# A fused convolution, attention and expert kernel: attention's sums are kept by channel and divided after a DRAM round trip, and three small turns move to VectorE

## The chip, the cores and the metric

The kernel runs on one core of a Trainium2 chip. The time is the device time of one execution in microseconds, as the median of the runs taken. A core has TensorE (PE, matrix products; weight loads are listed apart as PEld), VectorE (DVE), ScalarE (ACT, activations), GpSimd (POOL) and SyncE (SP), each with its own in-order queue. Here SP issues nearly all DMAs. TensorE writes to PSUM; VectorE and ScalarE read it from there.

## The reference

Layer 0 convolves twice, gates, and adds an attention with one head; layer 1 is attention with 16 heads of 8 channels, a gated feed-forward part and a router that mixes two of eight experts. All of it is float32.

```python
x: (4, 64, 64, 128)                       # 4 images, 4096 tokens, 128 channels
# layer 0
c1 = conv3x3(elu(x), W1) + b1;  c2 = conv3x3(c1, W2) + b2
a, b = split(c2);  c3 = a * sigmoid(b)
q, k, v = c3 @ Wq + bq, c3 @ Wk + bk, c3 @ Wv + bv       # 4, 4, 16 channels
probs = softmax(q k' / 4 under a strict lower triangle)
x = x + c3 + tile(probs @ v, 8) @ W3 + b3
# layer 1, t = tokens of x
h0 = ln(t)
q, k, v = h0 @ wq, h0 @ wk, h0 @ wv       # 16 heads of 8 channels
attn = softmax(q k') v                    # over all 4096 tokens of the image
h = h0 + attn @ wo
t = t + h + silu(h @ w1) * (h @ w3) @ w2
y = ln(t)
p = softmax(y @ router_w + router_b);  the two largest, scaled to sum 1, are the gates
t = t + sum over the chosen experts of gate * (y @ expert_w[e] + expert_b[e])
```

## The kernel before

**Names.** A chunk is 512 tokens (`QB`), 8 chunks to an image (`NQ`), 32 tiles of 128 keys (`NT`). The 16 heads of layer 1 are treated in four groups (`NG1`) of four slots (`NSLOT`), each slot having 32 partitions (`SLOT`).

**The long loop.** `attention_step` handles one tile of 128 keys for one chunk of queries and one group: 4096 steps in all. `scores()` issues four products (one per head, each on its own 32 rows of the array) into two PSUM tiles `s` (three buffers), and ScalarE exponentiates each tile of 128x1024 into `e`. `values()` issues four products with 9-column weights `vg` into the one accumulator `acc`: in each slot row 0 gathers the sum of the exponentials, rows 1 to 8 the weighted values. `values` run two steps behind `scores` (`finish(2)`).

After the last key tile VectorE copies `acc` to `at` (channels on partitions). Then `by_token` is put on the list `urgent`: TensorE turns `at` in four 128x128 transposes into PSUM tile `m`, VectorE takes the reciprocal of the sums (`rc`), multiplies (`nt`) and SP stores 32 channels per token in DRAM tensor `a`. With the last group, `last_part` is put on `fillers`.

**Fillers.** All other work is written as generators that yield a cost and a word; the main loop calls `insert` at most once per step, between the scores of the step and older values, as long as `credit` is above zero. The credit grows by a rate worked out from the work and steps left, and falls by the yielded cost. A yield of 0.0 is thus a pause of one step. `urgent` work goes first and counts 0.6. The list is served in order, one generator until it ends. The generators are `first_attention` (convolutions, first layer's attention, second layer's operands of the next image) and `last_part` (what follows attention, per chunk). All use the PSUM tile `m`, of which there is one; beside the loop, `product` cuts weights into 32 columns so that four products fill four column strips of the array. First-layer attention has its own steps (`first_step`) in the same loop.

`InOrder` keeps every engine's instructions in the order in which they are written.

**`last_part` before.** It loads `nt`, `h`, `t` for a chunk, pauses three steps, turns `nt` with four transposes, copies to `an`, multiplies by `wo1`, and goes on to the feed-forward part. After the second layer norm it turns `y`, multiplies by the router weights `rw` (four products with 128x128 weights, 8 columns moving), finds the gates on VectorE after an exponential `pr` on ScalarE, pauses four steps, turns the gates with four transposes into `g8` (experts on partitions), multiplies by the expert biases `eb`, and then forms all eight experts, `by_e`, in halves.

**First values before.** In `first_attention`, `wv0` is multiplied with `c3` as 128x128 weights and 16 moving columns, so that tokens are on partitions at once.

**Start and end.** Ahead of the loop (`alone`) the generators run beside each other without it, with `s` tiles for PSUM. The small weights are loaded by `weight(...)` in one run on SP's queue. After the loop the rest of the fillers runs alone: what is left of chunk 6 and all of chunk 7 of the last image.

All engine calls pass through one helper, so the profile gives one line number, L105, for all; the groups are told apart by tile names.

Of the kernel before, what the change touches and what calls it, by code (L numbers as in the profile page):

```python
# [15 lines left out]
P = 128  # L16
# [99 lines left out]
def fast_path(ctx: ExitStack, tc: tile.TileContext, a: dict, where: dict, out: bass.AP, verdict):  # L116
# [102 lines left out]
    seen = const.tile([P, 4, B], FP, name="f_seen")  # L219


    steps_in, undone, fillers, urgent = [], [], [], []
    held, turn = [False], [0]

    def do_step(step):
        scores, values = step
# [7 lines left out]
    def advance(part):  # L234

        r = next(part[0], None)
        part[1] = max(0.5, part[1] - (r[0] if r else 0.0))
        held[0] = r is not None and r[1] in ("held", "rounds")
        return r

    def insert():

        if urgent and not held[0] and turn[0] > urgent[0][0]:
            urgent.pop(0)[1]()
            return 0.6
        while fillers:
            r = advance(fillers[0])
            if r is not None:
                return r[0]
            fillers.pop(0)  # L250
        return 0.0
# [25 lines left out]
    def product(ps, lhsT, rhs, start=True, stop=True):  # L277

        m = lhsT.shape[1]
        size = m if alone[0] else SLOT  # L280
        for lo in range(0, m, size):
            hi = min(lo + size, m)
            pe.matmul(ps[lo:hi], lhsT=lhsT[:, lo:hi], rhs=rhs, start=start, stop=stop)

    def halves(ps, lhs, rhs, size=P):

# [240 lines left out]
    def first_attention(b, st):  # L527
# [3 lines left out]
        for c in range(NQ):  # L531
            while len(st.done) <= c:

                yield (0.0, "wait") if alone[0] else next(st.conv, (0.0, "stop"))
            while alone[0] and st.second < c - 1:
                yield 0.0, "wait"
            c3 = st.done[c]
            t = xt
            pool.tensor_tensor(by_k(t), by_k(t), b3.unsqueeze(1).to_broadcast([P, 4, C]), ALU.add)
            if c + 1 < NQ:  # L540
                xt = load_x(b, c + 1, "xt")

            ps = bank()
            yield from halves(ps, wq0, c3)
            u, qx0 = chunk("u"), chunk("qx0")
            dve.tensor_scalar(u, ps, bq0, 0.25, ALU.add, ALU.mult)
            dve.tensor_reduce(top0[:, 0, c : c + 1], u, AX.X, ALU.max, apply_absolute_value=True)
            two_terms(u, qx0, "q")
            yield 0.46, "stop"
            ps = bank()  # L550
            for j in range(NSLOT):
                pe.matmul(
                    ps[j * SLOT : (j + 1) * SLOT, :P],
                    lhsT=wk0,
                    rhs=c3[:, j * P : (j + 1) * P],
                    start=True,
                    stop=True,
                )
            yield 0.25, "held"
            for k in range(4):  # L560
                pe.matmul(
                    ps[:, P + k * DV0 : P + (k + 1) * DV0],
                    lhsT=c3[:, k * P : (k + 1) * P],
                    rhs=wv0,
                    start=True,
                    stop=True,
                )
            u = chunk("u")[:, :P]
            dve.tensor_scalar(u, ps[:, :P], bk0, None, ALU.add)
            v0c = v0[:, 4 * c : 4 * c + 4, 1 : 1 + DV0]  # L570
            dve.tensor_tensor(
                v0c,
                ps[:, P : P + 4 * DV0].rearrange("p (k s) -> p k s", s=DV0),
                bv0.unsqueeze(1).to_broadcast([P, 4, DV0]),
                ALU.add,
            )
            dve.tensor_reduce(top0[:, 1, c : c + 1], u, AX.X, ALU.max, apply_absolute_value=True)
            dve.tensor_reduce(
                top_v0[:, c : c + 1],
                v0[:, 4 * c : 4 * c + 4, :].rearrange("p k s -> p (k s)"),  # L580
                AX.X,
                ALU.max,
                apply_absolute_value=True,
            )
            two_terms(u, kx0[:, c, :], "k")
            yield 0.95, "stop"

            ps = bank()
            transposed(c3, ps)
            dve.tensor_tensor(t, ps, t, ALU.add)  # L590
            yield 0.6, "stop"

            while alone[0] and st.read < c:
                yield 0.0, "wait"
            sums, found = [], []
            for r in range(c + 1):
                steps_in.append(first_step(c, r, qx0, sums, found))
            while not found:
                yield 0.0, "rounds"
            st.ready.append((t, found[0]))  # L600
            while not alone[0] and st.second <= c:
                yield from second_operands(b, st)
# [173 lines left out]
    def attention_step(b, seg, kt, place, qx, vg, part):  # L776
# [19 lines left out]
        def values(es):  # L796
# [8 lines left out]
            if kt == seg.hi - 1:  # L805
                at = chunk("at1")
                if part:
                    dve.tensor_tensor(at, acc, part[0], ALU.add)
                else:
                    dve.tensor_copy(at, acc)  # L810
                if seg.hi == NT:
                    urgent.append((turn[0] + 1, lambda: by_token(b, g, c, at)))
                else:
                    sp.dma_start(out=scratch[b]["p"][g, c], in_=at)

        return scores, values

    def by_token(b, g, c, at):

        ps = m_tile()  # L820
        transposed(at, ps)
        pj = ps.rearrange("p (k j s) -> p k j s", j=NSLOT, s=SLOT)
        rc = sm.tile([P, 4, NSLOT], FP, tag="rc", name="rc")
        dve.reciprocal(rc, pj[:, :, :, 0])
        nt = sm.tile([P, 4, NSLOT, HD1], FP, tag="nt", name="nt")
        dve.tensor_tensor(
            nt, pj[:, :, :, 1 : 1 + HD1], rc.unsqueeze(3).to_broadcast([P, 4, NSLOT, HD1]), ALU.mult
        )
        gc = slice(g * NSLOT * HD1, (g + 1) * NSLOT * HD1)
        sp.dma_start(out=scratch[b]["a"][c][:, :, gc], in_=nt.rearrange("p k j d -> p k (j d)"))  # L830
        if g == NG1 - 1:
            fillers.append([last_part(b, c), LAST])


    def last_part(b, c):
        d = scratch[b]
        t, h, nt = chunk("xt", "t"), chunk("xe", "h"), chunk("pos", "nt")
        sp.dma_start(out=by_k(nt), in_=d["a"][c])
        sp.dma_start(out=h, in_=d["h"][c])
        sp.dma_start(out=t, in_=d["t"][c])  # L840
        for _ in range(3):
            yield 0.0, "stop"
        ps = bank()
        transposed(nt, ps)
        an = chunk("pos", "an")
        dve.tensor_copy(an, ps)
        yield 0.6, "stop"
        ps = bank()
        tokens(ps, an, wo1, range(2))
        yield 0.46, "held"  # L850
# [45 lines left out]
        dve.tensor_copy(yT, ps)  # L896
        yield 0.6, "stop"
        ps = bank()
        for k in range(4):
            pe.matmul(  # L900
                ps[:, k * NE : (k + 1) * NE], lhsT=yT[:, k * P : (k + 1) * P], rhs=rw, start=True, stop=True
            )
        shape = [P, 4, NE]

        def over(ap):
# [2 lines left out]
        def top(score, name):  # L908
# [10 lines left out]

        lg = small("lg", [4, NE])  # L920
        dve.tensor_tensor(
            lg, ps[:, : 4 * NE].rearrange("p (k e) -> p k e", e=NE), rb.unsqueeze(1).to_broadcast(shape), ALU.add
        )
        m0 = small("m0", [4])
        dve.tensor_reduce(m0, lg, AX.X, ALU.max)
        dve.tensor_tensor(lg, lg, over(m0), ALU.subtract)
        pr = small("pr", [4, NE])
        yield 0.95, "stop"
        act.activation(pr, lg, AF.Exp)
        yield 0.0, "stop"  # L930
        yield 0.0, "stop"
# [5 lines left out]
        dve.tensor_tensor(w1, w1, pr, ALU.mult)  # L937
        dve.tensor_tensor(m1, m1, m2, ALU.add)
        dve.reciprocal(m1, m1)
        gate = small("gate", [4, NE])  # L940
        dve.tensor_tensor(gate, w1, over(m1), ALU.mult)
        for _ in range(4):
            yield 0.0, "stop"

        ps = bank()
        for k in range(4):
            pe.transpose(ps[:NE, k * P : (k + 1) * P], gate[:, k, :], ident)
        g8 = chunk("at0", "g8")[:NE]
        dve.tensor_copy(g8, ps[:NE, :])
        yield 0.6, "stop"  # L950
        ps = bank()
        tokens(ps, g8, eb, range(2))
        yield 0.46, "held"
# [25 lines left out]
    class Batch:  # L979


        def __init__(self, b):
# [4 lines left out]
                "k": [P, 2, N],  # L987
                "q": [NQ, P, 2, 2, QB],
                "v": [NG1, P, NQ, 4 * NSLOT * (1 + HD1)],
                "a": [NQ, P, 4, C],  # L990
            }
            if b == 0:
                dims["p"] = [NG1, NQ, P, QB]
# [36 lines left out]
    def weight(name, src, shape):  # L1030
        w = const.tile(shape, FP, name="f_" + name)
        sp.dma_start(out=w, in_=src)
        return w


    n_row = 4 * DQK0

# [19 lines left out]
    wk0 = repeated("wk0", a["L0_conv_Wk"], 1)  # L1057
    bq0 = repeated_bias("bq0", a["L0_conv_bq"])
    bk0 = repeated_bias("bk0", a["L0_conv_bk"])
    wv0 = weight("wv0", a["L0_conv_Wv"], [P, DV0])  # L1060
    bv0 = weight("bv0", a["L0_conv_bv"].partition_broadcast(P), [P, DV0])
    b3 = weight("b3", a["L0_conv_b3"].partition_broadcast(P), [P, C])

# [16 lines left out]
    fw2 = const.tile([P, len(FCH), C], FP, name="f_fw2")  # L1080
    for n, (lo, size) in enumerate(FCH):
        sp.dma_start(out=fw2[:size, n, :], in_=a["L1_attn_w2"][lo : lo + size, :])
    rw = weight("rw", a["L1_ffn_router_w"], [P, NE])
    rb = weight("rb", a["L1_ffn_router_b"].partition_broadcast(P), [P, NE])
    we = weight("we", a["L1_ffn_expert_w"].rearrange("e d c -> d e c"), [P, NE, C])
    we_f = we.rearrange("p e c -> p (e c)")
# [100 lines left out]
    steps = stream()  # L1187
    credit, waiting = 0.0, False
    while True:
        turn[0] += 1  # L1190
        if steps_in:
            do_step(steps_in.pop(0))
        else:
# [15 lines left out]
            within = steps_left[b] - 40 if b + 1 < B else min(steps_left[b] - 40, 160)  # L1209
            rate = sum(us for _, us in fillers) / max(1, within)  # L1210
        credit = min(0.7, credit + rate)
        if waiting or credit > 0.0 and not quiet[0] or urgent and not held[0]:
            credit -= insert()
        finish(2)
    finish(0)
    while urgent:
        if held[0]:
            advance(fillers[0])
        else:
            urgent.pop(0)[1]()  # L1220
    alone[0] = True
    run_alone([(r for part in fillers for r in part[0])], lambda: False)

# [716 lines left out]
```

## Time and profile before

| | us |
|---|---|
| median of 3 runs | 8293.93 (8293.24 to 8297.26) |
| profiled execution, whole | 8302.43 |
| its span | 8300.7 |

Busy time of the engines in the span, by stretch (start of the span to 415 us: start; to 8225: the loop; then the tail):

| stretch | PE | DVE | ACT | POOL |
|---|---|---|---|---|
| 415 to 8225 (7810 us) | 7746.7 | 2272.6 | 7727.6 | 559.0 |
| whole span (8300.7 us) | 8073.1 | 2557.3 | 7915.4 | 708.5 |

TensorE's granted clock is 0.98 of full speed over the span and 1.00 in the loop. A group's row of the profile gives line, engine, operation, out<-in by the program's names, shapes and count, then busy time and mean duration in ns, then idle time ahead of it with what ended it. A pipelined matmul's duration overlaps that of its neighbours, so time per step is read from start to start. The groups that the change touches:

```profile
L105 ACT ACTIVATE e<-s 128x1024 f32<-128x1024 f32 x8424 | 7813.0, 1088 | 132.6 <-PE s L105 123.5 <-ACT e L105 1.5 <-issue 1.5
L105 PE MATMUL m<-f_consts,at 128*128 128x128 f32 x512 | 84.0, 287 | 1.2 <-DVE at L105 1.2
L105 PE MATMUL m<-f_rw,y2T 128*128 128x8 f32 x248 | 32.8, 259 | 0.0
L105 PE MATMUL m<-f_wv,c 128*128 128x16 f32 x240 | 32.1, 266 | 0.0
L105 PE MATMUL m<-f_consts,nt 128*128 128x128 f32 x124 | 20.4, 288 | 3.3 <-DMA nt<-d_a 3.0
L105 PE MATMUL m<-f_consts,gate 128*8 128x128 f32 x124 | 18.6, 273 | 0.0
```

The DMAs near it, with size and median time from issue to landing:

```profile
d_a<-nt SPq DMA_DIRECT2D x128, 64.0 KB, 2.1
nt<-d_a SPq DMA_DIRECT2D x32, 256.0 KB, 2.9
h<-d_h SPq DMA_DIRECT2D x32, 256.0 KB, 3.1
```

### The profile page before, as it was taken

The page shows a single profiled execution, that of the slowest core. Times are in us where ns is not written, and L with a number is a line of the kernel's source. Part 1 is how long each engine was busy: PE and PEld are TensorE (multiplying, and loading weights), DVE is VectorE, ACT ScalarE, POOL GpSimd, SP SyncE. Part 2 cuts the span into 40 slices and gives each one's busy share as a digit, 9 for nine tenths or more (in the row PEclk, how much of TensorE's full clock was granted, in tenths as well). Part 3 has the DMA queues.
Part 4 walks back from the last instruction along what each step waited for, and adds up shares of the span by engine and source line. Part 5 has one row for each costly group of instructions (what it writes and reads, how often), then busy time and mean ns, then how long its engine had stood idle before and what let it go on. Part 6 is the DMA issues. An engine that isn't in the chain of part 4 may idle for free.

```text
span 8300.7 us, 173662 instructions
## 1 busy us (share of the span) xinstructions
PE 8073.1 (97%) x73713; PEld 2576.8 (31%) x73713; DVE 2557.3 (31%) x5278; ACT 7915.4 (95%) x8699; POOL 708.5 (9%) x597
## 2 busy tenths in 40 slices
PE   5899999999999999999999999999999999999998
PEld 3223222223333332333333333233333333332333
DVE  7333122223322223333322222333333223221223
ACT  1799999999999999999999999999999999999996
POOL 5101111000000002111000000211000000000000
PEclk7899999999999999999999999999999999999998
DMA  1222001101100001001010000101111111111110
GB/s 56 70 70 66 19 27 36 36 27 49 41 23 14 21 18 32 22 30 47 33 38 11 27 15 19 30 27 39 42 37 40 33 39 42 38 33 34 59 55 30
DMA packets 239541, 295.99 MB, mean 36 GB/s; under 512 B 81731, under 2 KB 153891, under 8 KB 238755
## 3 DMA queue, kind: packets, MB, share of 16 engines
q1 hardware_dynamic: 234739, 283.03, 10.6%
q8 instruction: 580, 9.50, 0.5%
q10 hardware_dynamic: 4016, 1.77, 0.1%
q14 instruction: 206, 1.69, 0.1%
HBM read 185.12 MB, written 99.61 MB: 34 GB/s over the span
## 4 chain that ended last, share of the span: by engine, by line
PE 87%; issue 7%; DVE 3%; ACT 1%; POOL 1%; DMA 1%; SPq 0%; ACTq 0%; POOLq 0%; DVEq 0%
PE acc L105 41%; PE s L105 28%; PE m L105 18%; ACT e L105 1%; DVE h L105 1%; DVE added L105 0%; DMA nt<-d_a 0%; DVE t L105 0%; POOL v L105 0%; DMA f_kx<-d_k 0%; POOL rs L105 0%; DVE two L105 0%; DMA xe<-in_x_dram 0%; DVE at L105 0%; DVE by_e L105 0%
## 5 line engine op out<-in xcount | busy, mean ns | idle before, releaser
L105 ACT ACTIVATE e<-s 128x1024 f32<-128x1024 f32 x8480 | 7842.5, 1087 | 133.4 <-PE s L105 124.3
L105 PE MATMUL acc<-e,vg 128*9 128x512 f32 x32768 | 4337.9, 595 | 1.7 <-DVE at L105 1.7
L105 PE MATMUL s<-qx,f_kx 32*128 32x512 f32 (+1 forms) x16960 | 2817.2, 495 | 46.5 <-ACT e L105 30.9
L105 PEld LDWEIGHTS s<-qx,f_kx 32*128 32x128 f32 (+1 forms) x16960 | 1128.1, 182 | 4046.7 <-ACT e L105 3788.7
L105 PEld LDWEIGHTS acc<-e,vg 128*9 128x9 f32 x32768 | 711.1, 90 | 784.0 <-issue 446.5
L105 PE MATMUL m<-v,f_wino 128*32 128x256 f32 x5328 | 431.5, 397 | 6.0 <-DVE t L105 3.5
L105 DVE TENSOR_TENSOR by_e<-m,gate 128x512 f32<-128x512 f32 x244 | 168.8, 692 | 725.7 <-PE m L105 725.7
L105 POOL TENSOR_TENSOR v<-r 128x1024 f32<-128x1024 f32 x128 | 248.5, 1947 | 1180.2 <-PE m L105 1159.9
L105 POOL TENSOR_TENSOR rs<-ve,f_minus_half 128x4 f32<-128x4 f32 x64 | 65.2, 1019 | 2997.6 <-DVE ve L105 2957.3
L105 PE MATMUL m<-f_we,y2T 128*32 128x256 f32 x3904 | 311.8, 391 | 2.3 <-DVE nt L105 2.3
L105 DVE COPY sd<-m 128x512 f32<-128x512 f32 x166 | 114.9, 692 | 570.8 <-PE m L105 570.8
L105 DVE COPY at<-acc 128x512 f32<-128x512 f32 x130 | 89.9, 692 | 555.8 <-PE acc L105 555.8
L105 DVE TENSOR_REDUCE added<-by_e 128x128 f32<-128x1024 f32 x128 | 255.3, 1995 | 4.4
L105 POOL TENSOR_TENSOR t<-t,h 128x512 f32<-128x512 f32 x32 | 40.9, 1277 | 2443.6 <-DVE h L105 2443.6
L105 PE MATMUL m<-hT,f_fw 128*32 128x256 f32 (+1 forms) x2728 | 236.1, 391 | 0.0
L105 DVE TENSOR_TENSOR t<-m,sums 128x256 f32<-128x256 f32 x126 | 53.5, 425 | 435.1 <-PE m L105 435.1
L105 DVE TENSOR_TENSOR t<-m,t 128x512 f32<-128x512 f32 x62 | 42.9, 692 | 455.6 <-PE m L105 455.6
L105 DVE SCALAR_TENSOR_TENSOR h<-m,h 128x512 f32<-128x512 f32 (+1 forms) x93 | 64.2, 690 | 372.9 <-ACT th L105 249.1
L105 DVE COPY h<-m 128x512 f32<-128x512 f32 (+1 forms) x93 | 64.2, 690 | 317.9 <-PE m L105 317.9
L105 PEld LDWEIGHTS m<-v,f_wino 128*32 128x32 f32 x5328 | 106.6, 109 | 173.5 <-issue 144.6
L105 PE MATMUL m<-e,f_v 128*32 128x512 f32 (+2 forms) x1128 | 152.2, 585 | 0.0
L105 DVE TENSOR_TENSOR e<-e,f_consts 128x128 f32<-128x128 f32 x128 | 30.2, 296 | 321.5 <-ACT e L105 321.5
(259 smaller groups left out, 3775.8 us busy)
## 6 DMA issues: line engine op xcount, KB each, us to landing
f_kx<-d_k SPq DMA_DIRECT2D x139, 512.0 KB, 4.0
qx<-d_q SPq DMA_DIRECT2D x152, 256.0 KB, 2.8
d_q<-two SPq DMA_DIRECT2D x64, 512.0 KB, 3.6
vg<-d_v SPq DMA_DIRECT2D x32, 576.0 KB, 4.2
d_k<-two SPq DMA_DIRECT2D x32, 512.0 KB, 3.4
d_v<-vc SPq DMA_DIRECT2D x32, 288.0 KB, 2.8
xe<-in_x_dram SPq DMA_DIRECT2D x32, 256.0 KB, 2.9
xt<-in_x_dram SPq DMA_DIRECT2D x32, 256.0 KB, 3.7
```

Source lines behind the costliest of these rows:

```text
L105: made = op(*args, **kw)
```

## The change

- `by_token` and the list `urgent` go. `at` is stored in DRAM as it is, 128 channels by 512 tokens per group (`a` grows to that shape).
- `last_part` reads from there the sums (`rs`, row 0 of each slot, laid out as 128x64) and the eight value rows of each head (`an`, 128x512). After three pauses VectorE takes the reciprocals, which go to DRAM tensor `r` and come back spread over the eight channels of each head (`per`). After four more pauses `an` is multiplied by `per`, and one pause later goes into the product with `wo1`.
- Router and first values: `few_by_token` takes the weights, zero-padded to 32 columns (`few_columns`), as the stationary operand and moves 128 tokens over each of four column strips, in such an order of tokens that VectorE's transpose of 32x32 blocks brings them to tokens on partitions.
- The gates are made in a tile padded to 32, turned in blocks by VectorE (`turned`), stored in DRAM tensor `g` and read back in four pieces as `g8`. The four pauses ahead of it become six.
- The costs yielded after router and first values fall from 0.95 to 0.24.

```diff
+    def few_by_token(ps, weights, src):
+        tokens_of = src.rearrange("p (k b a) -> p b k a", k=4, a=SLOT)
+        for b in range(4):
+            pe.matmul(ps[b * SLOT : (b + 1) * SLOT], lhsT=weights, rhs=tokens_of[:, b], start=True, stop=True)
...
-            for k in range(4):
-                pe.matmul(ps[:, P + k * DV0 : P + (k + 1) * DV0],
-                    lhsT=c3[:, k * P : (k + 1) * P], rhs=wv0, start=True, stop=True)
+            few_by_token(ps[:, P : 2 * P], wv0, c3)
+            few = sm.tile([P, 4, SLOT], FP, tag="few", name="few")
+            dve.transpose(few.rearrange("p k s -> p (k s)"), ps[:, P : 2 * P])
...
-                if seg.hi == NT:
-                    urgent.append((turn[0] + 1, lambda: by_token(b, g, c, at)))
-                else:
-                    sp.dma_start(out=scratch[b]["p"][g, c], in_=at)
+                to = scratch[b]["a"][c, g] if seg.hi == NT else scratch[b]["p"][g, c]
+                sp.dma_start(out=to, in_=at)
+                if seg.hi == NT and g == NG1 - 1:
+                    fillers.append([last_part(b, c), LAST])
...
-        sp.dma_start(out=by_k(nt), in_=d["a"][c])
+        heads = d["a"][c].rearrange("g (j s) n -> (g j) s n", s=SLOT)
+        rs = chunk("neg", "sums")[:, : QB // HD1]
+        sp.dma_start(out=rs, in_=heads[:, 0, :].rearrange("j (i n) -> j i n", i=HD1))
+        sp.dma_start(out=an, in_=heads[:, 1 : 1 + HD1, :])
         sp.dma_start(out=h, in_=d["h"][c])
         sp.dma_start(out=t, in_=d["t"][c])
         for _ in range(3):
             yield 0.0, "stop"
-        ps = bank()
-        transposed(nt, ps)
-        an = chunk("pos", "an")
-        dve.tensor_copy(an, ps)
-        yield 0.6, "stop"
+        dve.reciprocal(rs, rs)
+        sp.dma_start(out=d["r"][c], in_=rs)
+        per = chunk("pos", "per")
+        sp.dma_start(
+            out=per, in_=d["r"][c].rearrange("(j i) n -> j (i n)", i=HD1).unsqueeze(1).to_broadcast([NH1, HD1, QB])
+        )
+        for _ in range(4):
+            yield 0.0, "stop"
+        dve.tensor_tensor(an, an, per, ALU.mult)
+        yield 0.0, "stop"
...
-        for k in range(4):
-            pe.matmul(ps[:, k * NE : (k + 1) * NE], lhsT=yT[:, k * P : (k + 1) * P], rhs=rw, start=True, stop=True)
+        few_by_token(ps[:, :P], rw, yT)
+        scores = sm.tile([P, 4, SLOT], FP, tag="few", name="scores")
+        dve.transpose(scores.rearrange("p k s -> p (k s)"), ps[:, :P])
...
+        pool.memset(gates[:, :, NE:], 0.0)
+        turned = chunk("w", "turned")[:, :P]
+        dve.transpose(turned, gates.rearrange("p k s -> p (k s)"))
+        sp.dma_start(out=d["g"][c], in_=turned)
+        g8 = chunk("at0", "g8")[:NE]
+        by_block = d["g"][c].rearrange("(b e) (k a) -> b e k a", e=SLOT, a=SLOT)
+        for b_ in range(4):
+            sp.dma_start(out=g8.rearrange("e (k b a) -> b e k a", k=4, a=SLOT)[b_], in_=by_block[b_, :NE])
+        for _ in range(6):
             yield 0.0, "stop"
-        ps = bank()
-        for k in range(4):
-            pe.transpose(ps[:NE, k * P : (k + 1) * P], gate[:, k, :], ident)
-        g8 = chunk("at0", "g8")[:NE]
-        dve.tensor_copy(g8, ps[:NE, :])
-        yield 0.6, "stop"
...
+    def few_columns(name, src):
+        w = const.tile([P, SLOT], FP, name="f_" + name)
+        pool.memset(w, 0.0)
+        sp.dma_start(out=w[:, : src.shape[1]], in_=src)
+        return w
...
-    wv0 = weight("wv0", a["L0_conv_Wv"], [P, DV0])
+    wv0 = few_columns("wv0", a["L0_conv_Wv"])
...
-    rw = weight("rw", a["L1_ffn_router_w"], [P, NE])
+    rw = few_columns("rw", a["L1_ffn_router_w"])
```

More of the change, by code (lines that the diff above doesn't have):

```diff
@@ L219, in fast_path @@
     seen = const.tile([P, 4, B], FP, name="f_seen")
-    steps_in, undone, fillers, urgent = [], [], [], []
-    held, turn = [False], [0]
+    steps_in, undone, fillers = [], [], []
     def do_step(step):
@@ L237, in advance @@
         part[1] = max(0.5, part[1] - (r[0] if r else 0.0))
-        held[0] = r is not None and r[1] in ("held", "rounds")
         return r
     def insert():
-        if urgent and not held[0] and turn[0] > urgent[0][0]:
-            urgent.pop(0)[1]()
-            return 0.6
         while fillers:
@@ L559, in first_attention @@
             yield 0.25, "held"
-            for k in range(4):
[L561 to L567, printed above, removed]
+            few_by_token(ps[:, P : 2 * P], wv0, c3)
+            few = sm.tile([P, 4, SLOT], FP, tag="few", name="few")
+            dve.transpose(few.rearrange("p k s -> p (k s)"), ps[:, P : 2 * P])
             u = chunk("u")[:, :P]
@@ L572, in first_attention @@
                 v0c,
-                ps[:, P : P + 4 * DV0].rearrange("p (k s) -> p k s", s=DV0),
+                few[:, :, :DV0],
                 bv0.unsqueeze(1).to_broadcast([P, 4, DV0]),
@@ L585, in first_attention @@
             two_terms(u, kx0[:, c, :], "k")
-            yield 0.95, "stop"
+            yield 0.24, "stop"
             ps = bank()
@@ L810, in values @@
                     dve.tensor_copy(at, acc)
-                if seg.hi == NT:
-                    urgent.append((turn[0] + 1, lambda: by_token(b, g, c, at)))
-                else:
-                    sp.dma_start(out=scratch[b]["p"][g, c], in_=at)
+                to = scratch[b]["a"][c, g] if seg.hi == NT else scratch[b]["p"][g, c]
+                sp.dma_start(out=to, in_=at)
+                if seg.hi == NT and g == NG1 - 1:
+                    fillers.append([last_part(b, c), LAST])
         return scores, values
[L818 to L832, printed above, removed]
     def last_part(b, c):
         d = scratch[b]
-        t, h, nt = chunk("xt", "t"), chunk("xe", "h"), chunk("pos", "nt")
-        sp.dma_start(out=by_k(nt), in_=d["a"][c])
+        t, h, an = chunk("xt", "t"), chunk("xe", "h"), chunk("pos", "an")
+        heads = d["a"][c].rearrange("g (j s) n -> (g j) s n", s=SLOT)
+        rs = chunk("neg", "sums")[:, : QB // HD1]
+        sp.dma_start(out=rs, in_=heads[:, 0, :].rearrange("j (i n) -> j i n", i=HD1))
+        sp.dma_start(out=an, in_=heads[:, 1 : 1 + HD1, :])
         sp.dma_start(out=h, in_=d["h"][c])
@@ L898, in last_part @@
         ps = bank()
-        for k in range(4):
-            pe.matmul(
-                ps[:, k * NE : (k + 1) * NE], lhsT=yT[:, k * P : (k + 1) * P], rhs=rw, start=True, stop=True
-            )
+        few_by_token(ps[:, :P], rw, yT)
+        scores = sm.tile([P, 4, SLOT], FP, tag="few", name="scores")
+        dve.transpose(scores.rearrange("p k s -> p (k s)"), ps[:, :P])
         shape = [P, 4, NE]
@@ L921, in last_part @@
         dve.tensor_tensor(
-            lg, ps[:, : 4 * NE].rearrange("p (k e) -> p k e", e=NE), rb.unsqueeze(1).to_broadcast(shape), ALU.add
+            lg, scores[:, :, :NE], rb.unsqueeze(1).to_broadcast(shape), ALU.add
         )
@@ L927, in last_part @@
         pr = small("pr", [4, NE])
-        yield 0.95, "stop"
+        yield 0.24, "stop"
         act.activation(pr, lg, AF.Exp)
@@ L939, in last_part @@
         dve.reciprocal(m1, m1)
-        gate = small("gate", [4, NE])
+        gates = sm.tile([P, 4, SLOT], FP, tag="few", name="gates")
+        gate = gates[:, :, :NE]
         dve.tensor_tensor(gate, w1, over(m1), ALU.mult)
-        for _ in range(4):
-            yield 0.0, "stop"
-        ps = bank()
-        for k in range(4):
-            pe.transpose(ps[:NE, k * P : (k + 1) * P], gate[:, k, :], ident)
-        g8 = chunk("at0", "g8")[:NE]
-        dve.tensor_copy(g8, ps[:NE, :])
-        yield 0.6, "stop"
+        pool.memset(gates[:, :, NE:], 0.0)
[7 more added lines that the diff above has]
+        for _ in range(6):
+            yield 0.0, "stop"
         ps = bank()
@@ L989, in __init__ @@
                 "v": [NG1, P, NQ, 4 * NSLOT * (1 + HD1)],
-                "a": [NQ, P, 4, C],
+                "a": [NQ, NG1, P, QB],
+                "r": [NQ, P, QB // HD1],
+                "g": [NQ, P, P],
             }
@@ L1189, in fast_path @@
     while True:
-        turn[0] += 1
         if steps_in:
@@ L1211, in fast_path @@
         credit = min(0.7, credit + rate)
-        if waiting or credit > 0.0 and not quiet[0] or urgent and not held[0]:
+        if waiting or credit > 0.0 and not quiet[0]:
             credit -= insert()
@@ L1215, in fast_path @@
     finish(0)
[L1216 to L1220, printed above, removed]
     alone[0] = True
```

## The prediction

> **What bounds the kernel now.** I read the page's first part, then the chain of waits, the groups by shape, and the timeline step by step.
>
> ```profile
> PE 8073.1 (97%) x73713; PEld 2576.8 (31%) x73713; DVE 2557.3 (31%) x5278; ACT 7915.4 (95%) x8699; POOL 708.5 (9%) x597
> ...
> PE 87%; issue 7%; DVE 3%; ACT 1%; POOL 1%; DMA 1%; SPq 0%; ACTq 0%; POOLq 0%; DVEq 0%
> ```
>
> TensorE and ScalarE both look full, and the chain lies on TensorE. The timeline tells which of the two is late in a step (one step: a group of `s` scores, what is inserted into `m`, a group of `acc` values, two exponentials):
>
> ```profile
> 2383.57 6.58 ACT L105 ACTIVATE e<-s 128x1024 f32<-128x1024 f32 x7
> ...
> 2387.60 0.50 PE L105 MATMUL s<-qx,f_kx 32*128 32x512 f32 x4
> 2388.03 0.97 PEld L105 LDWEIGHTS m<-f_rw,y2T 128*128 128x128 f32 x8 [0.24 <-issue]
> ...
> 2390.00 0.50 PE L105 MATMUL s<-qx,f_kx 32*128 32x512 f32 x4
> ...
> 2390.60 2.86 ACT L105 ACTIVATE e<-s 128x1024 f32<-128x1024 f32 x3 [0.45 <-PE s L105]
> 2391.41 0.46 PEld L105 LDWEIGHTS s<-qx,f_kx 32*128 32x128 f32 x4 [0.86 <-issue]
> ```
>
> With nothing inserted TensorE needs 1.41 us a step (2390.00 to 2391.41). Starts of exponentials, read one by one, stand 0.905 us apart when fed, so ScalarE needs 1.81. Inserts in 32-wide tiles make a step of 1.86 (653 Winograd steps and 487 expert steps have that median): even. **ScalarE sets the pace and idles only behind longer inserts**, here 0.45 us. So a gain must be ScalarE idle time won back. From 415 to 8225 us I added up what each start-to-start distance exceeds 0.905 (or 0.52 and 0.12 after the small activations): 232 us, the ceiling of the long stage.
>
> **What is removed.** The removed inserts use all 128 columns of the array. Score-to-score step medians, and the ScalarE idle in the 4.2 us that follow each:
> - router, `m<-f_rw,y2T`: 2.40 us; 19.2 us over 31
> - first values, `m<-f_wv,c`: 2.53; 15.4 over 30
> - `nt` transposes: 2.43; 11.0 over 31
> - gate transposes: 2.37; 7.9 over 31
> - `by_token` transposes, `m<-f_consts,at`: 2.00; 26.1 over 128.
>
> The sum is 79.6. Any other such stretch holds 4.3 exponentials with 15.6 ns of idle each (107.5 us over 6894), 0.067 us; 251 stretches, 16.8 us, would be there anyway. Rest: **62.8 us gained** (17.1, 13.4, 8.9, 5.9, 17.5). The transposes of `y` and `c3` next to them stay. VectorE's removed work (128 x (0.255+0.292) for `rc` and `nt`, 31 x 0.69 for `an`, 31 x 0.68 for `g`) is worth nothing: it is busy 31%.
>
> **What is added.**
> *Router and first values on TensorE.* Four products with 32-wide weights over 128 columns are what `m<-c,f_rwk` already is; its steps have a median of 1.65 us, under 1.81: no cost. Bounds of the insert: 0 and 0.45 us (that of 1.86).
> *Block turns on VectorE*, 92 of 128x128: no such row. The ends are 0.15 us (128x4 operations) and 0.69 (a 512-wide copy from PSUM); nearest is `nt<-m`, 128x128, 0.292: I take 0.3. Hidden, VectorE being idle two thirds of the time; uncovered, they delay the release of `m` by 0.3 (61 x 0.3 = 18 us at worst).
> [...] But the timed resource here is the TensorE slot: the row says 2.40 us for a step with the router[...].
> *Sums by DRAM.* `last_part` gets reads `rs` and `an`, a reciprocal, store `d_r`, read `per`, a multiply, against read `nt`, four transposes, a copy. Rows: 256 KB store 2.0 us, read 2.9. After the last values step of a chunk (time 0): copy `at` done 2.6, store 5.0, `rs` 8.1, reciprocal (0.18 for 128x4, 0.255 for 128x16; for 128x64 between 0.25 and 0.7, taken 0.4) 8.5, `d_r` 10.8, `per` 13.8, product 14.5. The pauses (three, four, one) put the first use of `an` on TensorE nine steps on, 9 x 1.81 = 16.3. Slack 1.8 us when nothing else fills the queue, more with a backlog. The reciprocal may hold VectorE for about 1 us (8.1 against four steps, 7.3); behind it stands no release of `m`, since fillers run one after another, and the next `at` copy is some 28 steps off.
> *Gates by DRAM.* In 20 of 31 rounds the gates are ready 5.3 us ahead of their transposes (4.6 at least). Written order gives `eb` nine steps after the router, two more than the transposes had: 5.3 + 3.7, less 0.9 (router step 0.6 shorter in pace, turn 0.3) = 8.1 us. Needed: turn 0.3, store `d_g` 2.1, three more issues of 0.4, landing 2.9, hops 0.2 = 6.7. Slack 1.4. A late `an` or `g8` would hold TensorE in order, with the next values and scores, and so ScalarE, behind it.
> [...] The old `d_a<-nt` is 64 KB in 128-byte pieces (128 partitions x 4), and lands in 2.1 us, as the 256 KB store in 2 KB pieces does in 2.0. [...]
> I book **4 us** for rounds in which a slack is missed (0 to 60: 62 waits of 1 us).
> *SP's queue.* Per chunk it gains two issues in front (`rs`, `an` for `nt`), `d_r`, `per`, `d_g`, four `g8`, and stands waiting for the reciprocal, `d_r`, the turned gates and `d_g`: about 5 us and 7 us. Behind it wait only `qx` and key quarters, asked for some 24 to 31 steps (over 40 us) ahead. POOL gets a memset per chunk, without a wait.
> *Pacing.* The written TensorE order has 2496 of 4237 steps filled, against 2683.
>
> **The start.** `few_columns` zeroes the tile on POOL before SP may load it, and POOL's queue is long there:
>
> ```profile
> 16.19 0.43 SPq L105 DMA_DIRECT2D f_wv<-in_L_conv_Wv_dram  x1
> ...
> 18.08 0.43 SPq L105 DMA_DIRECT2D qx<-in_L_conv_W_dram  x1
> ```
> ```profile
> 30.63 0.20 POOL L105 TENSOR_TENSOR f_bk<-f_bk,f_consts 128x4 f32<-128x4 f32 x1
> ```
> ```profile
> 30.94 0.28 DVE L105 COPY f_w3f<-s 128x128 f32<-128x128 f32 x1
> 31.14 0.42 DVE L105 TENSOR_SCALAR neg<-xe 128x512 f32<-128x512 f32 x1
> ```
>
> The memset comes after 30.83, so `f_wv` goes out at 31.0 instead of 16.19 and everything behind it on SP 14.8 us later. `qx` (W3) is issued at 32.9, lands 2.2 later, TensorE's product takes 0.77, and VectorE's in-order copy `f_w3f` ends at 36.1, not 31.2; all of VectorE's start work stands behind it. **+4.9 us.** The later `xt` and `xe` loads are needed at 42 and 71 us.
>
> **The tail.** After the loop nothing covers a DMA:
>
> ```profile
> 8234.82 2.79 DMA nt<-d_a
> 8237.75 1.10 PE s L105 x4
> 8238.87 0.70 DVE an L105
> ```
>
> Load to `wo`: 4.8 us now; 2.9+0.4+2.0+2.9+0.7+0.3 = 9.2 after: +4.4. Gates to `eb`: 1.95 (8272.48 to 8274.41) against 6.7: +4.7. Router: -1.0 (1.9 to about 0.9). Chunk 6 leaves three half expert blocks behind the loop, not four, and `by_token` goes: 6.3 us against 8.9, -2.6. **+5.5 us.**
>
> **Sum:** -62.8 + 4 + 4.9 + 5.5 = -48.4. The profiled execution took 8302.4 (span 8300.7), so about 8254; it stood 8.5 above the median of the runs. Against the median: 8293.9 - 48.4 = **8245.5 us**.
>
> **Rivals.**
> 1. *More is won.* With 187 fewer filled steps the remaining idle (107 us spread thinly) shrinks by a third too, and no slack is missed: -62.8 - 36 + 10.4 = -88, **8206**. For it: dense runs of 1.86 steps are where that idle lies. Against: the rows after the change are as long as before.
> 2. *Nothing measurable.* A measurement tells about 0.2%, 17 us, from no change. VectorE holds `m` for the turns (18 us) and half of the waits miss by 0.7 us (22 us): 8245.5 + 36 = **8282**.
> 3. *Slower: the DRAM round trips come onto TensorE's path.* If each store takes 4.1 us (the longest `d_a`) and each read 4.0 (the longest `nt` waits in the chain) instead of 2.1 and 2.9, a chain is 3.1 longer, 1.5 past its slack; 62 x 1.5 = 93: 8245.5 + 93 = **8339**. It turns the sign from about 0.8 us per wait. For it: six `nt` waits of the old kernel, 11.1 us in all. Against: the medians, and DMA engines 11% busy.
>
> **Chances:** forecast 0.62, rival 1 0.18, rival 2 0.10, rival 3 0.10. Range 8200 to 8284, which reaches rivals 1 and 2. Faster 0.82, within 0.2% 0.09, slower 0.09.
>
> **What would show it.** Router and first-value steps at or under 1.81 us; the number of ScalarE gaps cut by about 60 us in total; `f_wv` issued near 31 us and `f_w3f` copied near 36; `wo` in the tail 9 us after `rs` is issued. Waits of TensorE for DMA `per` or `g` in the middle would show rival 3; a turn much over 0.3 us rival 2.

## The result, and the profile after

| | before | after |
|---|---|---|
| median of the runs, us | 8294.64 (8293.24 to 8297.26, 4 runs) | 8255.74 (8252.75 to 8256.29, 4 runs) |
| span of the profiled execution | 8300.7 | 8254.1 |
| start: to the first step of the long loop | 211.2 | 217.7 |
| long loop: to its last values product | 8012.5 | 7954.1 |
| tail: from there to the end | 77.0 | 82.2 |

The ratio of the times is 0.9952 (95% interval 0.9935 to 0.9969): 38.9 us faster. Span against span it is 46.6, since the profiled execution of before took 8302.43, 7.8 above the median of the table, and that of after, 8256.29, lies at its own. The loop is counted here from its first step, not from the round 415 us of the table ahead.

The page of after, busy time of the engines and the chain of waits by engine:

```profile
PE 8010.7 (97%) x72957; PEld 2492.4 (30%) x72957; DVE 2513.9 (30%) x5118; ACT 7886.0 (96%) x8699; POOL 712.2 (9%) x631
...
PE 86%; issue 7%; DVE 3%; ACT 1%; DMA 1%; POOL 1%; SPq 0%; ACTq 0%; POOLq 0%; DVEq 0%
```

The shares are within a point of those of before: nothing here tells that anything changed. The groups by shape of after do (busy us, mean ns, then the idle time ahead and what ended it):

```profile
L105 ACT ACTIVATE e<-s 128x1024 f32<-128x1024 f32 x8424 | 7784.2, 1103 | 99.7 <-PE s L105 94.7 <-ACT e L105 1.3 <-issue 1.1
...
L105 DVE TENSOR_TENSOR an<-an,per 128x512 f32<-128x512 f32 x32 | 22.2, 692 | 210.7 <-DMA per<-d_r 210.7
...
L105 DVE RECIPROCAL sums<-sums 128x64 f32<-128x64 f32 x32 | 17.7, 552 | 85.0 <-DMA sums<-d_a 85.0
...
L105 PE MATMUL m<-y2T,f_rw 128*32 128x128 f32 x248 | 13.2, 285 | 0.0
...
L105 DVE STREAM_TRANSPOSE turned<-gates 128x128 f32<-128x128 f32 x32 | 10.0, 312 | 3.7 <-DVE gates L105 0.5
...
L105 DVE STREAM_TRANSPOSE few<-m 128x128 f32<-128x128 f32 x30 | 9.5, 317 | 32.2 <-PE m L105 32.2
```

In the first row read busy and idle time together, for exponentials overlap (1088 and 1103 ns each, 0.906 and 0.905 us from start to start by the median) and the rows split the overlap arbitrarily: 7813.0 + 132.6 before, 7784.2 + 99.7 now, 61.7 us less for the same 8424 exponentials. The DVE rows show where the DRAM round trip waits: 210.7 us of VectorE idle before the product with `per`, 6.6 a chunk, on an engine that is 30% busy. What matters is whether TensorE waits behind it. Its waits in the loop (420 to 8160 us; total, times, longest):

```profile
PE s L105 <- ACT e L105: 30.5, 52, 4.1
...
PEld m L105 <- DVE an L105: 3.2, 4, 1.7
...
PE m L105 <- DVE an L105: 1.9, 2, 1.4
```

The weight loads of `wo` wait for `an` four times, its products twice; nothing waits for `g`. And the router's step, in the timeline of after:

```profile
2447.02 10.27 ACT L105 ACTIVATE e<-s 128x1024 f32<-128x1024 f32 x11
...
2452.92 0.51 PE L105 MATMUL s<-qx,f_kx 32*128 32x512 f32 x4
...
2453.35 0.43 PE L105 MATMUL m<-y2T,f_rw 128*32 128x128 f32 x8
...
2453.85 0.32 DVE L105 STREAM_TRANSPOSE scores<-m 128x128 f32<-128x128 f32 x1 [1.11 <-PE m L105]
...
2454.57 0.52 PE L105 MATMUL s<-qx,f_kx 32*128 32x512 f32 x4
```

From scores to scores 1.65 us, and ScalarE runs through from 2447.02 to 2457.29: the 0.45 us gap of the old router step is gone.

The two ends grew. The start of after, SP's and POOL's rows and VectorE's copy of W3:

```profile
30.97 0.12 POOL L105 MEMSET f_wv<- 128x32 f32 x1
31.12 0.33 SPq L105 DMA_DIRECT2D f_wv<-in_L_conv_Wv_dram  x1
...
32.92 0.43 SPq L105 DMA_DIRECT2D qx<-in_L_conv_W_dram  x1
...
36.80 0.29 DVE L105 COPY f_w3f<-s 128x128 f32<-128x128 f32 x1 [5.57 <-PE s L105]
```

and its tail, sums first, gates after:

```profile
8180.43 0.59 SPq L105 DMA_DIRECT2D sums<-d_a  x1
...
8182.56 0.55 DVE L105 RECIPROCAL sums<-sums 128x64 f32<-128x64 f32 x1 [2.64 <-DMA sums<-d_a]
8183.14 0.32 SPq L105 DMA_DIRECT2D d_r<-sums  x1
...
8186.16 0.53 SPq L105 DMA_DIRECT2D per<-d_r  x1
...
8190.32 2.05 PE L105 MATMUL s<-f_wo,an 128*128 128x128 f32 x8 [15.09 <-DVE an L105]
...
8221.88 0.31 DVE L105 STREAM_TRANSPOSE turned<-gates 128x128 f32<-128x128 f32 x1
8222.22 0.32 SPq L105 DMA_DIRECT2D d_g<-turned  x1
8223.82 2.88 SPq L105 DMA_DIRECT2D g<-d_g  x4
...
8228.09 2.04 PE L105 MATMUL s<-f_eb,g 8*128 8x128 f32 x8 [11.07 <-DMA g<-d_g]
```

The copy is 5.9 us later than before. Load to `wo` is 8180.43 to 8190.32, 9.9 us against 4.8; gates to `eb` 8221.77 (end of the gates' multiply) to 8228.09, 6.3 against 1.93.

### The profile page after: what moved, and what is told of

Its sections match the earlier page's. It is cut to its first block, busy times and chain, and to the rows that moved or that the text cites. A ratio compares the mean times of both kernels' runs of the same rounds, so it can differ in the third digit from the quotient of the medians.

```text
span 8254.1 us, 172356 instructions
## 1 busy us (share of the span) xinstructions
PE 8010.7 (97%) x72957; PEld 2492.4 (30%) x72957; DVE 2513.9 (30%) x5118; ACT 7886.0 (96%) x8699; POOL 712.2 (9%) x631
## 3 DMA queue, kind: packets, MB, share of 16 engines
q10 hardware_dynamic: 4016, 1.77, 0.1%
## 4 chain that ended last, share of the span: by engine, by line
PE 86%; issue 7%; DVE 3%; ACT 1%; DMA 1%; POOL 1%; SPq 0%; ACTq 0%; POOLq 0%; DVEq 0%
PE acc L105 41%; PE s L105 29%; PE m L105 16%; ACT e L105 1%; DVE h L105 1%; POOL v L105 0%; DVE t L105 0%; DMA xe<-in_x_dram 0%; DMA f_kx<-d_k 0%; SPq L105 0%; POOL rs L105 0%; DMA d_r<-sums 0%; DVE added L105 0%; DVE sums L105 0%; POOL xt L105 0%
## 5 line engine op out<-in xcount | busy, mean ns | idle before, releaser
L105 ACT ACTIVATE e<-s 128x1024 f32<-128x1024 f32 (+1 forms) x8480 | 7813.8, 1101 | 100.5 <-PE s L105 95.5
L105 PE MATMUL s<-qx,f_kx 32*128 32x512 f32 (+2 forms) x16960 | 2918.2, 496 | 49.2 <-ACT e L105 33.5
L105 PEld LDWEIGHTS s<-qx,f_kx 32*128 32x128 f32 (+1 forms) x16960 | 1168.8, 182 | 4105.3 <-ACT e L105 3882.9
L105 DVE TENSOR_TENSOR by_e<-m,gates 128x512 f32<-128x512 f32 x245 | 169.5, 692 | 682.0 <-PE m L105 682.0
L105 ACT ACTIVATE sd<-s 128x512 f32<-128x512 f32 x26 | 15.5, 597 | 118.8 <-DVE t L105 60.8
```

The costliest lines, as they stand in the source:

```text
L105: made = op(*args, **kw)
```

## The experiments

All times are medians; each ratio is to the kernel before, run beside it on the same chip.

**Which part brings what.** Four kernels take one part out of after.

`e1_late_pads` loads the two padded weights behind all others:

```diff
-    wv0 = few_columns("wv0", a["L0_conv_Wv"])
...
-    rw = few_columns("rw", a["L1_ffn_router_w"])
...
+    wv0 = few_columns("wv0", a["L0_conv_Wv"])
+    rw = few_columns("rw", a["L1_ffn_router_w"])
```

> The changed kernel with one edit: the two padded weights (wv0, rw) are loaded behind all other small weights, so SP no longer stands at the POOL memset before W3 is loaded. Theory A (part of the late start is absorbed: in the changed kernel the first loop step starts 6.5 us later than before, but step 64 only 3.3 and step 128 only 2.7): the f_w3f copy is back near 31.2 us and the first loop step comes 6 us earlier, but the whole time falls by only 2 to 4 us, to 8252-8254. Rival B (my prediction: the shift goes through whole): -5 to -6, 8250. Rival C (it is all absorbed): 8255.7, no change.

8249.93 us, ratio 0.9943 (0.9929 to 0.9956). The copy `f_w3f` is back at 31.29 us, the first loop step at 214.0 instead of 217.7, 3.7 us of the 6 that theory A had; the span is 2.8 us shorter. By the times alone the two kernels can't be told apart, since the intervals of their ratios overlap; the start can. Over the traces of all runs below it falls into groups: 217.7 to 219.1 with the padded loads where after has them (after, e2, e4, e7, e8, e11, e12), 211.6 to 214.4 with them last (e1, e5, e6, e9, e10), 211.2 and 211.5 without them (before, e3). The place of two small loads costs the start about 5 us (means 218.4 and 213.1).

`e2_gates_tensor` gives the gates back to TensorE:

```diff
-        turned = chunk("w", "turned")[:, :P]
-        dve.transpose(turned, gates.rearrange("p k s -> p (k s)"))
-        sp.dma_start(out=d["g"][c], in_=turned)
...
-        for _ in range(6):
+        for _ in range(4):
             yield 0.0, "stop"
+        ps = bank()
+        for k in range(4):
+            pe.transpose(ps[:NE, k * P : (k + 1) * P], gate[:, k, :], ident)
+        g8 = chunk("at0", "g8")[:NE]
+        dve.tensor_copy(g8, ps[:NE, :])
+        yield 0.6, "stop"
```

> The changed kernel with the gate turns back on TensorE (four transposes, a copy, four pauses), all else as changed. Theory A (the idle that I booked to the gate transposes belonged to the expert-bias products that follow in the same window): loop time the same within 3 us, tail 4.2 us shorter (gates to eb 1.95 instead of 6.2): 8251.5. Rival B (windows as in my prediction): loop +5.9, tail -4.2: 8257.4. Rival C (the gate round trip costs in the loop, late g8): loop shorter by 10 or more, under 8246.

8245.28 us, ratio 0.9938 (0.9924 to 0.9951); by span 9.4 us shorter than after, 4.3 of it in the loop and 6.2 in the tail, less 1.1 at the start. The intervals of the two ratios overlap, but the slowest run of e2 (8246.6) is below the fastest of after (8252.8). The gates' way through DRAM loses. In the tail 4.4 us are the chain itself (6.3 against 1.93). Where the 4.3 in the loop come from isn't shown: ScalarE's idle time behind gates and `eb` is larger in e2 (12.5 against 10.8 us, see below).

`e3_wide_products` gives router and first values their 128-wide weights and yields of 0.95 back:

```diff
...
-        few_by_token(ps[:, :P], rw, yT)
-        scores = sm.tile([P, 4, SLOT], FP, tag="few", name="scores")
-        dve.transpose(scores.rearrange("p k s -> p (k s)"), ps[:, :P])
+        for k in range(4):
+            pe.matmul(ps[:, k * NE : (k + 1) * NE], lhsT=yT[:, k * P : (k + 1) * P], rhs=rw, start=True, stop=True)
...
-        yield 0.24, "stop"
+        yield 0.95, "stop"
...
```

> The changed kernel with router and first values as 128x128 weights and 8 or 16 moving columns again (costs yielded 0.95 again, no padding, so no late start). Theory A (ScalarE idle counted over whole groups, 20.2 to 1.1 and 16.6 to 1.9 us): loop +34, tail +1, start -3: 8288. Rival B (windows as predicted, 17.1 + 13.4): +30.5 +1 -5 = 8282. Rival C (the gain is pacing and fewer filled steps, not these products): within 5 of 8255.7.

8290.78 us, ratio 0.9994 (0.9985 to 1.0002); the loop is 37.6 us longer than after's. The edit changes the yields too, so rival C, that the pacing made the gain, has to be ruled out. ScalarE's idle time behind the two groups does it: counted as in the table of "Why the prediction came out as it did", it is 20 us behind the router and 17 behind first values, as in the kernel before, against 1 and 2 in after. That is some 33 of the 37.6. These 61 steps are the largest part of the gain.

`e4_sums_tokens` gives the sums back to `by_token`, with `urgent` and the transposes of `nt` (the tiles `few` and `nt` with one buffer each):

```diff
+                if seg.hi == NT:
+                    urgent.append((turn[0] + 1, lambda: by_token(b, g, c, at)))
...
-        dve.tensor_tensor(an, an, per, ALU.mult)
-        yield 0.0, "stop"
+        ps = bank()
+        transposed(nt, ps)
+        an = chunk("pos", "an")
+        dve.tensor_copy(an, ps)
+        yield 0.6, "stop"
...
```

> The changed kernel with attention's sums divided by token again (by_token on the urgent list, nt transposes), router, first values and gates as changed; nt and few have one buffer for want of room. Theory A (groups: by_token 19.8 to 0, nt and wo together 13.8 to 12.4): loop +21, tail -2: 8275. Rival B (windows as predicted, 17.5 + 8.9): +26.4 - 1.8: 8280. Rival C (the DRAM way costs as much as it saves): within 5 of 8255.7.

8277.58 us, ratio 0.9977 (0.9968 to 0.9986); loop 21.2 longer than after's, tail 2.7 shorter. Taken as differences of the ratios times 8294, the parts are: products 35 us gained (with the later start that their padding brings), sums 21 gained, gates 12 lost; 44 together against 40 measured.

**The version the parts point to.** `e5_best_two` has the edits of e1 and e2.

> The changed kernel with both edits that gained: padded weights loaded last (e1) and the gate turns on TensorE (e2). Theory A (they act at start and end and are independent): e1 gained 2.8 us of span (3.7 at the first loop step), e2 9.4 (6.2 of it behind the loop, 4.3 in it): 12.2 in sum, 8243.5; against the kernel before a ratio near 0.9932. Rival B (one of the two was scatter between executions): within 4 of e2 alone, 8245 to 8249.

8236.66 us, ratio 0.9933 (0.9919 to 0.9946), below both kernels, and the ratio that theory A had (0.9932). Start 211.6, loop 7947.2, tail 75.9.

**What a missed slack costs.** `e6_direct_sums` is e5 without the round trip over `r`: the sums are read spread over the channels, and VectorE takes the reciprocal of 128x512. The four pauses go with it.

```diff
-        rs = chunk("neg", "sums")[:, : QB // HD1]
-        sp.dma_start(out=rs, in_=heads[:, 0, :].rearrange("j (i n) -> j i n", i=HD1))
+        per = chunk("pos", "per")
+        sp.dma_start(out=per, in_=heads[:, 0:1, :].to_broadcast([NH1, HD1, QB]))
...
-        dve.reciprocal(rs, rs)
-        sp.dma_start(out=d["r"][c], in_=rs)
...
-        for _ in range(4):
-            yield 0.0, "stop"
+        dve.reciprocal(per, per)
         dve.tensor_tensor(an, an, per, ALU.mult)
```

> As e5, and the sums are read from DRAM spread over 8 channels at once (128x512), so that VectorE takes 512 reciprocals per partition in place of 64 and the store d_r, its read and four pauses go. Theory A: the reciprocal takes 3.4 us (128x64 took 0.55, 128x4 0.18, so 6.2 ns an element); behind the loop load to wo falls from 9.9 to 2.3+3.4+0.7+0.2 = 6.6, -3.3, and the 5 us of TensorE waits for an in the loop go, -3: 8237. Rival B (the long reciprocal holds VectorE in order while acc or m waits for it): loop 5 us or more longer than e5, 8243 or more.

8347.15 us, ratio 1.0064 (1.005 to 1.0077). The tail is 4.9 us shorter than e5's, the loop 119.4 us longer, far over rival B's 5 or more. TensorE's waits in the loop of e6:

```profile
PE m L105 <- DVE an L105: 77.8, 28, 4.4
```

The reciprocal takes 3.35 us. The chain from the last values of a chunk (copy, store, read, reciprocal, product) was left five steps, 9 us, and needs about 12: an estimate from the prediction's 8.1 to the landed sums, 3.35 and 0.7. But the waits are 77.8 us and the loss is 119.4. To see a small wait, `e7_sums_2_pauses` takes two of after's four pauses ahead of the product, and `e8_gates_4_pauses` two of its six ahead of `eb`:

```diff
# e7
-        for _ in range(4):
+        for _ in range(2):
             yield 0.0, "stop"
         dve.tensor_tensor(an, an, per, ALU.mult)
# e8
-        for _ in range(6):
+        for _ in range(4):
             yield 0.0, "stop"
```

> The changed kernel with two pauses instead of four between storing the reciprocals and the product an x per. In the changed kernel the product was done 0.05 to 6.8 us (median 2.0) before its first use by TensorE; two steps less are 3.6 us. Theory A (the pauses are what hides the round trip; rival 3 of the prediction names this as what turns the sign): about 24 of 31 rounds come late, by 55 us in sum, of which ScalarE's lead covers up to 0.9 each: +30 to +55, 8286 to 8311. Rival B (ScalarE's lead covers it all): 8256 +- 4.

> The changed kernel with four pauses instead of six between the gates and the expert-bias products. The last read of g8 was issued 4.75 us ahead of them, and lands 2.05 after its issue (behind the loop), so 2.7 us were to spare; two steps less are 3.6. Theory A: each of 31 rounds comes 0.9 us late, 28 us in sum, of which ScalarE's lead takes nearly all: +0 to +10, 8256 to 8266. Rival B (no lead is left at that point): +28, 8284. Rival C (shorter last_part, fewer steps left behind the loop): -4.

e7: 8316.18 us, ratio 1.0026 (1.0016 to 1.0036), 5 over theory A; loop 62.1 longer than after's, with 38.5 us of waits in 21 rounds. e8: 8336.03 us, ratio 1.0047 (1.0032 to 1.0063), loop 86.9 longer, far over anything expected, and TensorE's waits for the gates are:

```profile
PE m L105 <- DMA g<-d_g: 9.2, 31, 0.7
```

9.2 us of waits against 87 us of loop: the price is not the wait itself. One round of e8, first TensorE in the timeline, then the busy time of each engine and TensorE's granted clock (column PEclk; 1.00 is full speed) by stretch:

```profile
4571.75 1.05 PE L105 MATMUL acc<-e,vg 128*9 128x512 f32 x8
...
4574.46 0.62 PE L105 MATMUL m<-f_eb,g 8*32 8x128 f32 x10 [0.35 <-DMA g<-d_g]
...
4577.61 1.90 PE L105 MATMUL acc<-e,vg 128*9 128x512 f32 x8
...
4581.02 1.93 PE L105 MATMUL acc<-e,vg 128*9 128x512 f32 x8
...
4583.79 1.04 PE L105 MATMUL acc<-e,vg 128*9 128x512 f32 x8
```

```profile
core 0: us, PE busy (x) PEld busy (x) DVE busy (x) ACT busy (x) POOL busy (x), PEclk, DMA share, GB/s
4560.00:4576.00 16.00, 15.61 (x129) 4.44 (x124) 4.31 (x22) 15.85 (x19) 0.00 (x0) 1.00 0.03 6
4576.00:4583.00 7.00, 7.00 (x56) 1.81 (x52) 0.69 (x1) 3.88 (x4) 0.00 (x0) 0.51 0.01 2
4583.00:4594.00 11.00, 11.00 (x108) 3.35 (x108) 3.70 (x4) 10.50 (x12) 0.00 (x0) 1.00 0.00 0
```

The wait is 0.35 us. In the seven microseconds behind it the clock is 0.51, the values products take 1.9 us instead of 1.04, and ScalarE works 3.88 of 7. The table takes every round of `eb` (from 1.5 us before to 12 after) or `wo` (4.5 before) in the loop and adds ScalarE's idle time (what its start-to-start distances exceed, as in the prediction), apart for rounds with and without a stretch of half clock, called a spell, in that window:

| kernel, round | rounds with a spell | mean idle, us | rounds without | mean idle, us |
|---|---|---|---|---|
| after, `eb` (no waits) | 0 | | 31 | 0.57 |
| e8, `eb` | 18 | 4.69 | 13 | 1.07 |
| after, `wo` (4 short waits) | 1 | 3.49 | 30 | 0.51 |
| e7, `wo` | 13 | 4.49 | 18 | 1.00 |
| e6, `wo` | 22 | 5.45 | 9 | 0.98 |

A round without a spell costs about half a microsecond more than one of after, one with a spell four to five. For e8: 18 x 4.1 + 13 x 0.5 = 80 of the 87 us. The same sum gives 61 of the 62 us of e7 and 113 of the 119 of e6, so little is left for another cause. The loop of after has 58 us at half clock in all, that of e8 198.

`e11_gates_5_pauses` takes only one of the six pauses away:

```diff
-        for _ in range(6):
+        for _ in range(5):
             yield 0.0, "stop"
```

> after with five instead of six pauses ahead of eb; its slack was about 2.7 us at six, so 0.9 at five. Theory A (the loss of e8 comes from TensorE having to wait, however briefly, and from the lower clock that follows): no waits for g, some 12 half-clock spells as in after, time 8254 (8248 to 8262). Theory B (the loss grows with each pause taken away, waits or not): about half of e8's loss, time 8290 to 8305, with some 20 spells.

8255.9 us, ratio 0.9955 (0.9941 to 0.9968), as after. TensorE's waits for the gates are now:

```profile
PEld m L105 <- DMA g<-d_g: 1.4, 3, 0.5
...
PE m L105 <- DMA g<-d_g: 0.5, 2, 0.3
```

Two of its 31 rounds have a spell behind `eb`, and both had a wait. The loss is not proportional to pauses; it begins where the wait begins.

`e9_direct_sums_covered` gives e6 four pauses between the reciprocal and the product:

```diff
         dve.reciprocal(per, per)
+        for _ in range(4):
+            yield 0.0, "stop"
         dve.tensor_tensor(an, an, per, ALU.mult)
```

> e6_direct_sums with four pauses between the 128x512 reciprocal and the product, so that the product with wo comes nine steps after the reads again, as in e5_best_two. Theory A (e6 lost because 12 us of chain stood against 9 us of pauses, and the waits of TensorE brought half-clock spells): loop as in e5 (7947, +-4), TensorE waits for an near 0, some 12 half-clock spells, tail near 71; time 8232 (8226 to 8240). Theory B (the 3.2 us reciprocal on VectorE, or the spread read of the sums, is itself the loss): loop above 8000, time above 8285.

8234.15 us, ratio 0.9926 (0.9913 to 0.994): 113 us from e6 by four empty steps a chunk. No wait for `an` is left, the loop is 7945.9, and 9 spells of half clock (47.8 us) stand against 31 (157.0) in e6. So neither the long reciprocal nor the spread read was the loss. The tail is 75.0, not the 71 that I expected: e6 had most of that from its fewer pauses, not from the missing round trip: behind its loop 32 of TensorE's expert products are left, behind those of e5 and e9 40. Whether e9 beats e5 is open; their intervals overlap.

`e10_sums_6_pauses` gives e5 two more pauses ahead of the product:

```diff
-        for _ in range(4):
+        for _ in range(6):
             yield 0.0, "stop"
         dve.tensor_tensor(an, an, per, ALU.mult)
```

> e5_best_two with six pauses instead of four between the reads and the product with the reciprocals. Theory A (the 5 us of TensorE waiting for an, in few rounds, can be bought off by two more unfilled steps): waits for an 0, loop 0 to 8 us shorter, time 8233 (8228 to 8237). Theory B (two more unfilled steps per chunk push other inserts together, about 62 steps): loop 3 to 10 us longer, time 8240 to 8247.

8252.33 us, ratio 0.9948 (0.9934 to 0.9962), worse than both expectations. Its premise was wrong: e5 has no waits for `an` to buy off. Loop 8.3 us longer than e5's, as theory B has it, and tail 9.2 longer, which neither had: with two more pauses a chunk, more of the last fillers is left to run behind the loop, 60 expert products against 40. A pause isn't free either.

`e12_gates_4_filled` asks whether the clock falls only where thinly filled steps stand ahead of the wait. Each of e8's four pauses gets the router's small products once more, into a tile that nobody reads:

```diff
-        for _ in range(6):
+        for _ in range(4):
+            few_by_token(bank()[:, :P], rw, yT)
             yield 0.0, "stop"
```

> e8 (four pauses ahead of eb) with work in each of the four: the router's four small products once more into the free tile m, which nobody reads (a step with them had 1.65 us, under ScalarE's 1.81, so the pace should not change by itself, and the gates arrive as late as in e8). Theory A (the clock falls when a wait follows steps in which TensorE is not full): waits for g as in e8, but only some 12 half-clock spells and a time of 8252 to 8272. Theory B (the wait by itself brings the clock down, whatever stands before it): some 30 spells, 8320 to 8345. Theory C (no wait at all any more because the filled steps take longer): no waits for g, about 8256.

8308.64 us, ratio 1.0012 (1.0005 to 1.0018): between the theories. The waits stayed:

```profile
PE m L105 <- DMA g<-d_g: 11.9, 34, 1.5
```

The rounds of `eb` with a spell fell from 18 of 31 to 9 of 31 (mean idle 4.73 us with, 1.33 without; 54 us above after in sum, and the loop is 53 longer). So what TensorE did before the wait seems to count, as far as one trace of each can tell, but filling four steps doesn't remove the spells; some steps further ahead were still unfilled. How full they would have to be stays open.

## Why the prediction came out as it did

The forecast was 48.4 us gained; 46.6 came span to span, 38.9 by the medians. The mechanism holds: ScalarE's idle time behind wide inserts was the time to be had. From 418 us to the last values product its start-to-start excess fell from 231.7 to 177.2 us. (These sums, and the 232 of the prediction, come out with 0.907 us from start to start; with the 0.905 written there both are some 17 higher.) By the groups of the forecast, each less 15.6 ns an exponential:

| us of ScalarE idle | before | after | gained | forecast |
|---|---|---|---|---|
| router | 20.2 | 1.1 | 19.1 | 17.1 |
| first values | 16.6 | 1.9 | 14.7 | 13.4 |
| `by_token` | 19.8 | 0 | 19.8 | 17.5 |
| `nt`, `wo` | 13.8 | 12.4 | 1.4 | 8.9 |
| gates, `eb` | 11.8 | 10.8 | 1.0 | 5.9 |

That the loop was hit to 0.4 us (58.8 forecast, with the waits; 58.4 found) is in part luck. The first three terms of the table came out 5.6 larger in sum and the last two 12.4 smaller, the 4 us booked for waits are inside the measured groups, and 2.4 us were gained outside of them.

- **Router, first values, `by_token`** were a little better than forecast. Step medians are 1.65 us with the router and 1.77 with first values, under 1.81 as said. Going by the 2.40 us row is confirmed by e3 for the products' turns: there the wide products leave ScalarE 20 and 17 us of idle time again, against 1 and 2. For the gates, keeping the turn on TensorE was the better choice (e2, 8245.28 us against 8255.74).
- **`nt` and gates are the terms that were mis-sized**: 14.8 forecast, 2.4 found. I booked all idle in the 4.2 us behind the transposes to the transposes. The same window holds the two steps that follow, `wo` or `eb`, which were unchanged and are themselves over 1.81 us. Once the transposes were gone, `wo` and `eb` came behind unfilled steps, and their own medians rose (`eb` 1.98 to 2.18, `wo` 1.87 to 2.28). With the transposes given back they return: `eb` to 1.98 in e2, `wo` to 1.87 in e4. Why they rise is not shown. Undoing the gates leaves 12.5 in that group against 10.8.
- **The 4 us for waits** were about right: `an` was late four times (two of them show only at the weight loads), once with a spell of half clock, and that round had 3.49 us of idle against 0.51. The sums' slack was 2.0 us by the median (forecast 1.8), the gates' about 2.7 (forecast 1.4), an estimate: `eb` starts 4.75 us after the last read of `g` is issued, and in the tail, where it waits for that read, 2.05.
- **VectorE's turn** takes 0.31 to 0.32 us (0.3 taken), the reciprocal 0.55 (0.4 taken). Both stayed hidden.
- **The small pieces** of the DMAs, 128 bytes in `g8`, cost nothing that shows: in the tail `eb` starts 2.05 us after the last of the four reads of `g` is issued, where the prediction had 2.9 for a read. Booking no extra time for them, going by the old `d_a<-nt` (128-byte pieces, 2.1 us), was right.
- **Start** +6.5 against +4.9: the mechanism as worked out (5.9 at the copy), and about 5 by the groups of starts above; the rest is within their scatter.
- **Tail** +5.3 against +5.5, and the parts that can be read agree: load to `wo` +5.1 (4.4), gates to `eb` +4.4 (4.7), and 44 expert products left behind the loop instead of 48, which is chunk 6's three half blocks instead of four.
- **Rival 1** (denser loop wins more) fell: outside the windows of the groups ScalarE's idle is 15.8 ns an exponential, as before (15.5, counted the same way). **Rival 3** didn't come true in after, but its mechanism did in e6 to e8, and its price was too low: it counted a wait by its length, 1.5 us for 1.5 us. e8 paid about 2.8 us a round (87 over 31) for waits of 0.3. (Its sum also counts the 4 us booked for waits twice: 8335, not 8339.)

## What to carry to other kernels

A filler's cost in a loop that another engine paces is the excess of its own step over that pace (here router steps of 2.40 us against 1.81 left 20.2 us of idle time, those of 1.65 left 1.1), so book the idle behind a step to the one insert that overruns, and check whether its unchanged neighbours overrun too. A DRAM round trip in place of a transpose paid only while its consumers were reached with slack, and even then it needn't: the sums gained 21 us by it, and the gates lost 12 with no wait at all. A fraction of a microsecond short, and it lost several times what it missed (e8: 87 us of loop for 9.2 us of waits). Try one pause more and one less: on the short side lies a cliff (+60 and +80 us for two pauses fewer, e7 and e8), on the long side a slope that isn't free either (+16 us for two more, e10).

## What the hardware showed unexpectedly

Waits of TensorE of 0.2 to 0.7 us, behind steps with 1.41 us of work in 1.81, were followed by a granted clock of half for 3.4, 6.8 or 10.2 us in 18 of 31 rounds (e8). In the clock record of that trace every stretch of half clock begins on one grid of 3.413 us, to within 0.02 us over the whole run; so do those of after and before, each on its own grid. A wait of one length is followed by half clock in one round and not in another, as two rounds of e8 with waits of 0.40 us show:

```profile
2468.14 0.62 PE L105 MATMUL m<-f_eb,g 8*32 8x128 f32 x10 [0.40 <-DMA g<-d_g]
...
2471.11 1.90 PE L105 MATMUL acc<-e,vg 128*9 128x512 f32 x8
```
```profile
7164.69 0.62 PE L105 MATMUL m<-f_eb,g 8*32 8x128 f32 x10 [0.40 <-DMA g<-d_g]
...
7168.33 1.05 PE L105 MATMUL acc<-e,vg 128*9 128x512 f32 x8
```

The values products take 1.90 us behind the first and 1.05 behind the second. Why is not shown. No wait of TensorE's products for the gates in e8 was longer than 0.7 us; how much idle time goes with a fall of the clock can't be told from these runs.
